# Pacing two side streams by the matrix columns of their pieces, and two small matrix products given more rows or columns of the array

## The chip, the cores and the metric

The kernel runs on one core of a Trainium2 chip. The core has five engines with a queue each, and every queue runs its instructions in order: TensorE (PE in the profile, with its weight loads as PEld), VectorE (DVE), ScalarE (ACT), GpSimd (POOL) and SyncE (SP), which here issues the DMAs. The metric is the device time of one execution in microseconds (us). Before the change it is 24933.63 us, the median of three runs (24896.19 to 24951.63).

## The reference, cut to what matters

Sixty-four images of 96 x 28 x 28 pass through four layers, all in float32 unless a layer quantises.

- Layer 0: a router mixes four expert filters for each image; a 1x1 expansion to 576 channels, a 5x5 depthwise convolution, a squeeze gate and a 1x1 projection follow, with a residual.
- Layer 1: a normalisation, an input projection, a 3x3 depthwise convolution, and then a selective scan over the 784 positions in four directions, followed by a normalisation, a gate, an output projection and an MLP.
- Layers 2 and 3: a normalisation, mixing in the frequency domain (matrix products with cosines and sines), and a feed-forward layer with quantised operands.

The scan is the heart. For each image, direction k, channel d and state n it is

```python
dt = softplus(einsum('bkrl,kdr->bkdl', dts_r, dt_projs_w) + dt_projs_b)   # dts_r has 6 rows
hst = hst * exp(dt_t * A) + dt_t * B_t * x_t        # 784 steps
y_t = sum_n(hst * C_t)
```

## The kernel before, in words

The images are taken two at a time: 32 pairs. For each pair the scan is cut into 192 units of 128 lanes by 784 positions: 12 blocks (a direction and one of three channel tiles T) of 16 units. The method `run` writes the order of all the work out by hand; there is no scheduler behind it, so an engine's queue holds its instructions as `run` and the two generators below issue them.

**A unit** (the `recur` step of unit i) is one product on DVE, `pd = pb * u` (L903), and one scan on DVE (L907 forwards, L909 backwards). Its decays `da` are made by ACT four units ahead (`decay`, L91). POOL multiplies the result with `cs` (L986). After each group of four units PE sums them over the states into `yp` (`collect`, L925).

**pb** is the input row B spread over the lanes by PE (`spread_b`, L891). It has one buffer in the accumulator memory. A new one is needed at every fourth unit, and at every second one in the four blocks with T = 2: 64 times a pair. `spread_b` for unit i+1 is issued within unit i, so PE may only run it after DVE's product of unit i, and DVE's product of unit i+1 waits for it.

**The side streams** are generators that yield pieces of work for other pairs, woven into the units of the scan: stream a (`first_half`: layer 0 and layer 1 up to the inputs of the scan) for the pair after, stream b (`second_half`: the end of layer 1 and layers 2 and 3) for the pair before. The first pair's a runs alone ahead of the scan, the last pair's b alone after it. A piece ends with `yield 0`, the last one of a **window** with `yield 1`; stream a has 135 windows and b 153. Each stream has one accumulator bank (`bank_a`, `bank_b`), so a piece's next product waits until ACT or DVE has emptied the bank. Work that a piece wants to happen later, such as a DVE operation that reads its product, is put down with `after(n, run)` and issued at the start of the n-th window after it. Such DVE operations are L383 (the Newton step of a normalisation), L787, L1081, L1093, L1291 and L662.

The pace before is by count. From unit 6 of a pair on, each stream gets at most one window a unit, and `due` allows it while its share of windows is below its share of units. In the unit two ahead of a new pb (`fresh(i + 2)`, the **quiet** unit) a window is allowed only when the stream is four windows behind:

```python
quiet = fresh(i + 2)
due = lambda v: v.window * (per - 8) < (n - 5 - QUIET * quiet) * v.windows
advance([v for v in streams if not v.over and due(v)])
```

What is left at unit 191 is run out by `finish`.

**dt's projection** is in `first_half`, `steps`: for each of four directions and three tiles, two products (L824) of 12 weight rows (partitions 96 to 107) by 128 columns, each moving 12 x 392 values: 24 a pair. ACT empties each (Exp, then Ln for both halves), one bank for all. The 12 rows are written to a row tile by ACT at partitions 96 to 107 after the product L779; partitions 0 to 63 of the same tile hold remainders of B. **The centring** in `norm` (L358) and in `feed_forward` (L1313) multiplies 96 rows by the 96 x 96 matrix `center`, 32 products a pair.

A float32 product appears as two matmul records and moves each column four times; a product with 32 output rows shares the array with three others.

Of the kernel before, what the change touches and what calls it, by code (L numbers as in the profile page):

```python
# [73 lines left out]
QUIET = 4  # L74
# [49 lines left out]
class Stream:  # L124


    def __init__(self, pieces, windows):
        self.pieces, self.windows, self.window, self.later, self.over = pieces, windows, 0, {}, False
# [4 lines left out]

    def piece(self):

        if self.over:
            return False
        more = next(self.pieces, None)
        self.over = more is None
        return more == 0  # L140

    def begin(self):
        self.window += 1
        for run in self.later.pop(self.window, []):
            run()


def advance(streams):

    for v in streams:  # L150
        v.begin()
    going = list(streams)
    while going:
        going = [v for v in going if v.piece()]


class Model:
# [3 lines left out]
    def __init__(self, ctx, tc, a, out):  # L161
        self.tc, self.nc, self.a, self.out = tc, tc.nc, a, out
        self.act = Act(tc.nc)
        self.npairs = a["x"].shape[0] // 2
# [13 lines left out]
        self.setup()  # L178

# [31 lines left out]
    def setup(self):  # L211
# [48 lines left out]
        def folded(name, bias, gain, shift, pieces, w=None):  # L260
# [4 lines left out]
            for i, (rows, lo, hi) in enumerate(pieces):  # L265
                pt = fill("ab"[i % 2])
                nc.tensor.matmul(pt[rows, :1], w[:, lo:hi], shift, start=True, stop=True)
                nc.vector.tensor_add(bias[0][rows, bias[1](i)], bias[0][rows, bias[1](i)], pt[rows, :1])
            nc.vector.tensor_scalar_mul(w, w, gain)
            pt = fill("a")  # L270
            nc.tensor.matmul(pt[:C, : 4 * C], self.center, w, start=True, stop=True)
# [41 lines left out]
        for i in (2, 3):  # L313
# [7 lines left out]
            nc.tensor.matmul(pt[:C, :DI], self.center, w1[:C], start=True, stop=True)  # L321
# [29 lines left out]
    def norm(self, bank, images, sqs, rb, scratch):  # L351
# [3 lines left out]
        for b in range(2):  # L355
            for h in range(2):
                pt = self.bank(bank)
                nc.tensor.matmul(pt[:C, :HALF], self.center, images[b][:, cols(h)], start=True, stop=True)  # L358
# [3 lines left out]
        for g in range(4):  # L362
            nc.tensor.matmul(
# [44 lines left out]
    def conv_steps(self, pt, copied, rows, steps, weights, first, last):  # L408
        nc = self.nc
        for n, (x, y) in steps:  # L410
            for q in range(4):
                nc.tensor.matmul(  # L412
# [6 lines left out]
    def first_half(self, p, st):  # L419
# [23 lines left out]
        def expand(n, h):  # L443
            i, pe = order[n], bank()
            if i == 8:
                for b in range(2):
                    nc.tensor.matmul(
# [3 lines left out]
            else:  # L451
                c = i % 4
                nc.tensor.matmul(
# [17 lines left out]
        nc.tensor.matmul(ph[:24, :2], self.r_w1, pool, start=True, stop=True)  # L471
# [11 lines left out]
        for b in range(2):  # L483
            nc.tensor.matmul(pl[:, 4 * b : 4 * b + 4], hb[:, b, :], self.r_w2, start=True, stop=True)
# [36 lines left out]
        def mix(diag, of):  # L521
            pt = bank()
            for e in range(4):
# [5 lines left out]
                nc.tensor.matmul(o, diag[:, e, :], v, start=(e == 0), stop=(e == 3))  # L529
# [94 lines left out]
        for b in range(2):  # L624
            for c in range(5):
                rhs = self.mean_s[:, b : b + 1] if c == 4 else total[:, 4 * b + c : 4 * b + c + 1]
                nc.tensor.matmul(pz[:24, b : b + 1], self.se_w1[:, c, :], rhs, start=(c == 0), stop=(c == 4))
# [7 lines left out]
        for c in range(5):  # L635
            nc.tensor.matmul(pg[:, 2 * c : 2 * c + 2], se_w2[:, c, :], z, start=True, stop=True)
# [15 lines left out]
        for b in range(2):  # L652
            for h in range(2):
                pt = bank()
                for c in range(5):
                    w = self.wp_s[:, b, :] if c == 4 else wp[:, 4 * b + c, :]
                    v = src[8] if c == 4 else src[4 * b + c]
                    nc.tensor.matmul(pt[:C, :HALF], w, v[:, cols(h)], start=(c == 0), stop=(c == 4))
# [24 lines left out]
        def in_proj(T, z, h):  # L683
            base, pt = DI if z else 0, bank()
            if T < 2:
                nc.tensor.matmul(pt[:, :HALF], self.in_w[:, base : base + 128], xs[T][:, cols(h)], start=True, stop=True)
            else:
                for b in range(2):
                    nc.tensor.matmul(
# [72 lines left out]
        w_dt = k1[96:108, 1568:1952].rearrange("p (t n) -> p t n", t=3)  # L762
# [10 lines left out]
        def project_b(k):  # L773
            low[k] = self.rows_a.tile([128, L], F32, name="o")
            t, v = parts[k], low[k]
            for h in range(2):
                pt = bank()
                for T in range(3):
                    nc.tensor.matmul(  # L779
# [6 lines left out]
                act(v[96:108, cols(h)], pt[96:108, :HALF], AF.Copy)  # L786
# [9 lines left out]
        def project_c(odd):  # L796
            for h in range(2):
                pt = bank()
                for T in range(3):
                    nc.tensor.matmul(  # L800
# [15 lines left out]
        def steps(k):  # L816
# [3 lines left out]
            for T in range(3):  # L820
                dt, x = dts[T % 2], source[T]
                for h in range(2):
                    pt = bank()
                    nc.tensor.matmul(  # L824
                        pt[:, :HALF], w_dt[:, T, :], low[k][96:108, cols(h)], start=True, stop=True
# [60 lines left out]
    def spread_b(self, u):  # L886
# [3 lines left out]
        for lo, hi in SPANS:  # L890
            nc.tensor.matmul(self.pb[:, lo:hi], self.sel[:, self.image_of(u), u["g"], :], self.bs[u["k"]][:, lo:hi], start=True, stop=True)  # L891
# [20 lines left out]
    def collect(self, us):  # L912
# [5 lines left out]
        if u["k"] == 0 and u["g"] == 2:  # L918
            for lo, hi in SPANS:
                nc.tensor.matmul(  # L920
                    self.yp[:, lo:hi], self.diag_d[:, u["T"] // 2, :], self.x[:, lo:hi], start=False, stop=False
                )
        for lo, hi in SPANS:
            for j in range(4):
                nc.tensor.matmul(  # L925
# [13 lines left out]
    def run(self):  # L939
        nc, act = self.nc, self.act  # L940
        sts = [dict(p=p) for p in range(self.npairs)]
        self.rep, self.cs, self.bs, self.done, self.stored = {}, {}, {}, None, None
# [577 lines left out]
```

## Time and profile before

The profiled execution took 24965.63 us (its span is 24963.8 us, so 1.8 us lie around it), 32 us above the median of the runs.

| | value |
|---|---|
| mean granted TensorE clock | 0.804 |
| first product of the scan, from the page's start | the stretch 0 to 528 us holds stream a of the first pair alone |
| the first pair's 192 units (only a beside them) | 528 to 1147 us: 619 us |
| a pair in the middle (a and b beside it) | 5671 to 6425 us: 754 us |
| after the last unit (b alone) | 24462 to 24964 us: 502 us |
| ACT table loads | 1116 + 937, 1283 ns each |

The page lists, for each group of instructions, the line, engine, operation and tiles (output, then inputs), partitions x elements, how many, the busy time in us, the mean of one in ns, and then how long the engine stood idle ahead of them and who ended that wait. A table by stretches lists, for each stretch of time, the busy time of each engine with its count of instructions, the granted clock of TensorE (1.00 is full speed), the share of DMA and GB/s. The list of waits says who waited for whom: us in total, times, the longest.

### The profile page before, as it was taken

The numbers are of one execution on the slowest core, as the hardware profiler recorded it, in microseconds if no ns is written. First come the engines' busy times: TensorE is split into PE (matmuls) and PEld (weight loads), VectorE is DVE, ScalarE is ACT, GpSimd is POOL, SyncE is SP. The second block draws the span as 40 slices with busy tenths as digits, with TensorE's granted clock in tenths as the row PEclk, the third lists the DMA queues.
The fourth block names the chain that finished last, engine by engine and source line by source line (L and its number), as shares of the span: only waits on it lengthen the run. The fifth ranks groups of instructions, "written<-read, shape, count | busy, mean of one in ns | idle before, by whom it ended". The sixth has DMA issues, their size and how long they took to land.

```text
span 24963.8 us, 294265 instructions
## 1 busy us (share of the span) xinstructions
PE 19171.3 (77%) x102426; PEld 7075.6 (28%) x102426; DVE 19073.0 (76%) x15930; ACT 14204.9 (57%) x19706; POOL 15593.0 (62%) x9446
## 2 busy tenths in 40 slices
PE   5677777777777787777877777877777777777866
PEld 2232222232222232222322222322222322222322
DVE  1877877877877777777778777777777778787782
ACT  2565555555565655555655555655556555556542
POOL 1666666666666666666666666666666666666662
PEclk7788878788887788877888878888787888887865
DMA  4655555555555555555555555555555555555531
GB/s 127 202 176 178 180 182 171 173 175 184 178 179 173 174 171 180 181 171 172 172 178 178 181 171 174 173 179 180 178 175 173 174 183 178 173 177 176 171 124 37
DMA packets 1733050, 4263.16 MB, mean 171 GB/s; under 512 B 203140, under 2 KB 415396, under 8 KB 1731465
## 3 DMA queue, kind: packets, MB, share of 16 engines
q1 hardware_dynamic: 1731564, 4244.33, 54.8%
q8 instruction: 812, 13.30, 0.2%
q14 instruction: 674, 5.52, 0.1%
HBM read 3206.80 MB, written 882.59 MB: 164 GB/s over the span
## 4 chain that ended last, share of the span: by engine, by line
PE 46%; DVE 24%; ACT 16%; issue 5%; DMA 4%; SPq 2%; POOL 1%; DVEq 0%; ACTq 0%; POOLq 0%
PE bank_a L412 11%; DVE pd L903 7%; DVE h L907 7%; PE yp L925 6%; ACT slot L91 5%; DVE h L909 5%; PE bank_a L824 3%; ACT da L91 3%; DMA k<-padded 2%; ACT L91 2%; PE bank_b L1268 2%; PE bank_b L1206 2%; PE pb L891 2%; PE bank_b L358 2%; PE bank_a L779 2%
## 5 line engine op out<-in xcount | busy, mean ns | idle before, releaser
L986 POOL TENSOR_TENSOR h<-h,cs 128x784 f32<-128x784 f32 x6144 | 11389.8, 1860 | 5865.7 <-DVE h L909 1840.6
L903 DVE TENSOR_TENSOR pd<-pb,u 128x784 f32<-128x784 f32 x6144 | 6013.6, 979 | 2466.6 <-PE pb L891 2235.7
L91 ACT ACTIVATE da<-dt,c_A_logs 128x784 f32<-128x784 f32 x6144 | 5602.0, 940 | 2102.8 <-DVE h L907 1252.0
L907 DVE TENSOR_TENSOR_SCAN h<-da,pd 128x784 f32<-128x784 f32 x3072 | 5488.2, 1787 | 375.6 <-DVE pd L903 14.8
L909 DVE TENSOR_TENSOR_SCAN h<-da,pd 128x784 f32<-128x784 f32 x3072 | 5487.9, 1786 | 334.5 <-DVE pd L903 4.2
L412 PE MATMUL bank_a<-k,t 128*32 128x392 f32 x36864 | 3790.1, 540 | 411.6 <-DMA k<-padded 259.7
L925 PE MATMUL yp<-h,c_gather 128*32 128x512 f32 (+1 forms) x24576 | 3326.7, 636 | 186.0 <-POOL h L986 180.6
L91 ACT ACTIVATE slot<-bank_b 99x384 f32<-99x384 f32 (+4 forms) x2624 | 1286.1, 490 | 2779.9 <-PE bank_b L358 773.9
L891 PE MATMUL pb<-bsl,c_sel 96*128 96x512 bf16 (+1 forms) x4096 | 1221.4, 386 | 1424.7 <-DVE pd L903 1393.6
L412 PEld LDWEIGHTS bank_a<-k,t 128*32 128x32 f32 x36864 | 1071.2, 114 | 2531.2 <-issue 2340.2
L925 PEld LDWEIGHTS yp<-h,c_gather 128*32 128x32 f32 x24576 | 824.6, 129 | 2841.1 <-issue 2331.1
L91 ACT ACT_TABLE_LOAD x1116 | 1431.8, 1283 | 28.9 <-PE bank_a L412 3.3
L824 PE MATMUL bank_a<-o,k 12*128 12x392 f32 x1536 | 1031.1, 763 | 383.1 <-ACT k L91 187.2
L87 ACT ACT_TABLE_LOAD x937 | 1202.2, 1283 | 17.4 <-PEq L1509 0.7
L891 PEld LDWEIGHTS <-c_sel 96*128 96x128 bf16 x4096 | 314.8, 103 | 2594.0 <-DVE pd L903 1448.3
L91 ACT ACTIVATE o<-bank_a,bn_b,bn_s 128x392 f32<-128x392 f32 x576 | 390.1, 677 | 1123.0 <-PE bank_a L412 1112.4
L1206 PE MATMUL bank_b<-c_fwd,slot 99*96 99x197 f32 (+1 forms) x4096 | 910.9, 371 | 137.7 <-DVE slot L1229 63.6
L779 PE MATMUL bank_a<-r,k 128*108 128x392 f32 x1536 | 760.1, 626 | 314.1 <-DVE o L787 308.7
L91 ACT ACTIVATE slot<-bank_b,c_l_mix 96x393 f32<-96x393 f32 x768 | 467.0, 641 | 854.6 <-PE bank_b L1206 643.5
L358 PE MATMUL bank_b<-slot,c_center 96*96 96x392 f32 x1280 | 676.7, 616 | 289.0 <-ACT slot L91 158.1
L1268 PE MATMUL bank_b<-c_inv,slot 99*96 99x394 f32 x2048 | 863.7, 571 | 13.8 <-ACT slot L91 13.8
L412 PE MATMUL bank_a<-k,cv_diag 96*32 96x392 f32 x4608 | 659.7, 710 | 253.3 <-DMA k<-padded 194.8
(232 smaller groups left out, 22964.3 us busy)
## 6 DMA issues: line engine op xcount, KB each, us to landing
cs<-crow SPq DMA_DIRECT2D x2048, 392.0 KB
dt<-dt SPq DMA_DIRECT2D x1536, 392.0 KB
u<-u SPq DMA_DIRECT2D x1536, 392.0 KB
k<-padded SPq DMA_DIRECT2D x2304, 256.0 KB
padded<-pad SPq DMA_DIRECT2D x384, 592.0 KB
u<-k SPq DMA_DIRECT2D x384, 392.0 KB
k<-padded SPq DMA_DIRECT2D x576, 224.0 KB
out<-o SPq DMA_DIRECT2D x288, 392.0 KB
```

The source lines that it names most:

```text
L91: self.nc.scalar.activation(out, in_, func, **kw)
L412: nc.tensor.matmul(pt[32 * q : 32 * q + 32, :HALF].rearrange("p (h w) -> p h w", w=HW), weights(q, n), copied[:rows, q, y : y + 14, x : x ...
L779: nc.tensor.matmul(pt[:108, :HALF], w_b[:, k, T, :], source[T][:, cols(h)], start=(T == 0), stop=(T == 2))
L824: nc.tensor.matmul(pt[:, :HALF], w_dt[:, T, :], low[k][96:108, cols(h)], start=True, stop=True)
L891: nc.tensor.matmul(self.pb[:, lo:hi], self.sel[:, self.image_of(u), u["g"], :], self.bs[u["k"]][:, lo:hi], start=True, stop=True)
L903: nc.vector.tensor_mul(pd[:, :L], self.pb[:, :L], self.rep[(u["p"], u["blk"], "u4", u["j"])])
L907: nc.vector.tensor_tensor_scan(h, da, pd[:, :L], 0.0, ALU.mult, ALU.add)
L909: nc.vector.tensor_tensor_scan(h[:, ::-1], da[:, ::-1], pd[:, L - 1 :: -1], 0.0, ALU.mult, ALU.add)
L925: nc.tensor.matmul(self.yp[32 * j : 32 * j + 32, lo:hi], self.gather, us[j]["h"][:, lo:hi], start=first, stop=last)
L986: nc.gpsimd.tensor_mul(v["h"], v["h"], self.cs[self.key(v)])
L1206: nc.tensor.matmul(pt[:C, lo:hi], folded[k][:, c, at], self.fwd[:, 2 * k + c, : hi - lo], start=(c == 0), stop=(c == 1),)
L1268: nc.tensor.matmul(pt[:C, : 2 * NF].rearrange("p (a n) -> p a n", a=2), zo[b][:, 4 * part + n, :], m, start=(n == 0), stop=(n == 3),)
```

## The change

1. **Counting.** A helper `mm` issues every matmul and adds its columns to `self.work`: four for each float32 column, one otherwise, divided by four for products of up to 32 output rows and by two up to 64.
2. **Pacing.** `debt` is a running estimate of the columns that PE has still to do: each unit adds what was issued and takes off UNIT = 6800. A stream goes on piece by piece only while the debt is below ROOM = 3600 (a quarter of it in a quiet unit), or while the stream is more than LATE = 4 windows late. A window may so be spread over several units; a stream may run up to one window early. Stream a starts at unit 0 of a pair instead of 6; b still starts at 6.
3. **dt's projection** uses 108 weight rows: `dt_w` is padded with zeros to partitions 0 to 95, and all of partitions 0 to 107 of the row tile are the moving operand. ACT's copy fills partitions 64 to 107 instead of 96 to 107.
4. **The centring** uses 128 columns: `center` is padded with 32 zero columns; what reads the bank still reads 96 rows.

The diff, cut to its core (every other hunk only puts `self.mm` for `nc.tensor.matmul`):

```diff
-QUIET = 4
+LATE, UNIT, ROOM = 4, 6800, 3600
 class Stream:
-    def begin(self):
-        self.window += 1
-        for run in self.later.pop(self.window, []):
-            run()
+    def begin(self):
+        if not self.open:
+            self.open = True
+            self.window += 1
+            for run in self.later.pop(self.window, []):
+                run()
     def piece(self):
         more = next(self.pieces, None)
         self.over = more is None
-        return more == 0
+        self.open = more == 0
+        return self.open
+    def mm(self, out, weights, moving, **kw):
+        self.nc.tensor.matmul(out, weights, moving, **kw)
+        groups = 4 if out.shape[0] <= 32 else 2 if out.shape[0] <= 64 else 1
+        self.work += int(np.prod(out.shape[1:])) * (4 if moving.dtype == F32 else 1) / groups
...
-                nc.tensor.matmul(pt[:C, :HALF], self.center, images[b][:, cols(h)], start=True, stop=True)
+                self.mm(pt[:, :HALF], self.center, images[b][:, cols(h)], start=True, stop=True)
...
-        w_dt = k1[96:108, 1568:1952].rearrange("p (t n) -> p t n", t=3)
+        w_dt = k1[:108, 1568:1952].rearrange("p (t n) -> p t n", t=3)
-                act(v[96:108, cols(h)], pt[96:108, :HALF], AF.Copy)
+                act(v[64:108, cols(h)], pt[64:108, :HALF], AF.Copy)
-                        pt[:, :HALF], w_dt[:, T, :], low[k][96:108, cols(h)], start=True, stop=True
+                        pt[:, :HALF], w_dt[:, T, :], low[k][:108, cols(h)], start=True, stop=True
...
+        def advance(streams, room):
+            for v in streams:
+                v.begin()
+            while streams:
+                going = []
+                for v in streams:
+                    if room(v):
+                        if v.piece():
+                            going.append(v)
+                        self.debt += self.work
+                        self.work = 0
+                streams = going
...
-            if u and n >= 6:
-                quiet = fresh(i + 2)
-                due = lambda v: v.window * (per - 8) < (n - 5 - QUIET * quiet) * v.windows
-                advance([v for v in streams if not v.over and due(v)])
+            self.debt = max(0, self.debt + self.work - UNIT)
+            self.work = 0
+            if u:
+                late = {v: (n + 1 - v.start) * v.windows / (per - 2 - v.start) - v.window for v in streams}
+                limit = ROOM / 4 if fresh(i + 2) else ROOM
+                due = sorted((v for v in streams if not v.over and (v.open or late[v] > -1)), key=lambda v: -late[v])
+                advance(due, lambda v: self.debt < limit or late[v] > LATE)
```

## The prediction

> **What bounds the kernel now.** I read the page first: the busy line, and the groups of the scan.
>
> ```profile
> PE 19171.3 (77%) x102426; PEld 7075.6 (28%) x102426; DVE 19073.0 (76%) x15930; ACT 14204.9 (57%) x19706; POOL 15593.0 (62%) x9446
> ...
> L903 DVE TENSOR_TENSOR pd<-pb,u 128x784 f32<-128x784 f32 x6144 | 6013.6, 979 | 2466.6 <-PE pb L891 2235.7
> ...
> L907 DVE TENSOR_TENSOR_SCAN h<-da,pd 128x784 f32<-128x784 f32 x3072 | 5488.2, 1787 | 375.6 <-DVE pd L903 14.8
> L909 DVE TENSOR_TENSOR_SCAN h<-da,pd 128x784 f32<-128x784 f32 x3072 | 5487.9, 1786 | 334.5 <-DVE pd L903 4.2
> ```
>
> No engine is full. DVE carries the chain of the scan: a unit is 0.979 + 1.787 = 2.77 us, so a pair's 192 units are 531 us of pure scan. A middle pair takes 754 us (5671 to 6425), the first pair, without stream b, 619 us. What lies between is DVE's side work and DVE's waits. Next I read the list of waits of that middle pair, DVE alone (us in total, times, longest).
>
> ```profile
> DVE pd L903 <- PE pb L891: 73.3, 27, 8.5
> DVE slot L383 <- ACT slot L91: 15.4, 5, 8.8
> DVE slot L1093 <- PE bank_b L1121: 14.4, 4, 7.3
> DVE o L787 <- ACT o L91: 9.0, 4, 3.6
> DVE slot L1291 <- PE bank_b L1268: 5.2, 2, 3.6
> DVE slot L1081 <- PE bank_b L1037: 3.7, 2, 3.4
> DVE slot L1081 <- PE bank_b L1042: 3.1, 1, 3.1
> DVE slot L1081 <- DMA k<-padded: 3.1, 1, 3.1
> DVE r L662 <- PE bank_a L658: 2.0, 2, 1.0
> ```
>
> The reader sees 73.3 us of waiting for pb and 55.9 us (the other eight lines) for side results: 129 us in all, close to the gap between the two pairs. Both kinds end on PE's queue: pb stands behind side pieces, and a piece stands behind ACT, which empties its only bank. The same list for 6370 to 6427, where stream a makes dt, has one line, pb, with 19.5 us in 5 waits. The table by stretches says why.
>
> ```profile
> 6200.00:6220.00 20.00, 14.71 (x120) 6.00 (x118) 16.81 (x13) 13.92 (x19) 13.36 (x8) 0.99 0.66 194
> 6400.00:6420.00 20.00, 15.24 (x39) 4.36 (x31) 13.13 (x11) 15.20 (x25) 10.40 (x7) 0.50 0.55 183
> ```
>
> The first number after the span is PE's busy time, the third from the end the granted clock. PE is as busy in both, yet one runs at 0.99 and the other at 0.50. In the first PE runs mostly 96-row convolution products, four side by side; in the second mostly L824, with 12 of 128 rows. From the timeline of PE, one L824 product (two records) at full and at half clock:
>
> ```profile
> 6388.39 0.92 PE L824 MATMUL bank_a<-o,k 12*128 12x392 f32 x2 [0.68 <-ACT t L91]
> 6412.08 1.67 PE L824 MATMUL bank_a<-o,k 12*128 12x392 f32 x2 [0.68 <-ACT k L91]
> ```
>
> **The change part by part**, per middle pair; stream a stands beside 31 of the 32 pairs, stream b beside 31.
>
> *dt with 108 rows.* The moving columns stay the same. At half clock a window of two products costs 2 x (1.67 + 0.68) = 4.7 us, against 2.77 us of DVE work a unit, so pb falls behind; at full clock it is 2 x (0.92 + 0.68) = 3.2 us. In the stretch 6370 to 6427 about eight of the L824 products stand at 1.67: 8 x 0.75 = 6 us; three sums L925 at 2.84 against 1.52 us elsewhere: 4 us; the small products and the three pb beside them (0.83 or 0.86 against 0.49): 3 us. That is 13 of the 19.5 us of pb waits. Ends: 19.5 us won if all go; 3 us lost if the clock stays. The latter is the weight DMA: it grows from 12 to 108 rows, nine times the bytes, and PE's 93.9 us of waits for it (2.9 a pair) could double. I take 13 won and 1 lost for the DMA. A new wait on DVE's remainder (L787, rows 0 to 63) costs nothing: it is issued four or more windows earlier.
>
> The Trainium skill, "TensorE: Matmul & The Clock Gate", Part 1 (What's actually happening), says the clock follows how busy PE was lately. Taken as busy time that speaks against this edit: PE was busy 15.24 of 20 us at 0.50, rows would not matter, and the sum would lose its 13 us. The two stretches above contradict that reading, so the measurement decides. The same page, Part 3 (What overlaps and what doesn't), has weight loads overlap running products only when their row groups differ, which 108 rows would end. L453, 96 rows by 128 columns, takes 0.93 us for its two records at full clock, beside L824's 0.92, so the sum by the row has no charge for it.
>
> *The centring with 128 columns.* 32 products a pair, the same moving columns; L358's loads take 180 ns with 96 columns and L453's 198 with 128, so 64 x 18 ns = 1.2 us of loads, mostly ahead of their products. What it wins is bounded by L358's records at half clock (about 0.9 against 0.54 us for one, some 28% of them): 32 x 0.28 x 0.7 = 6 us of PE, off DVE's path. I take 0.
>
> *Pacing and DVE's side waits.* I counted float32 columns in the order in which the program issues them, side pieces alone, in a middle pair. Both kernels issue 754,836. Before, 27 of the 192 units get more than 9,300 (four us at full clock by the row: 3,136 columns of L412 take 1.53 us), after it 12. The longest single lump falls from 14,720 to 12,576, and the first 24 units get 59,234 instead of 46,690, since stream a starts six units earlier. A DVE operation put down with `after(1)` comes one unit, some 2.9 us, after its product; behind 9,300 columns it must wait. In the trace two thirds of the side waits (38 us) start within two units of such lumps. If they shrink with the lumps, 38 x 15/27 = 21 us go; I take 18. Ends: 55.9 won, 11 lost. The loss is ACT table loads: the program has 2331 instead of 2053, 8.7 more a pair at 1.283 us, and they stand in ACT's queue ahead of what L383 and L787 wait for. ACT is busy 446 of 754 us, so I charge a quarter in the sum, 3 us.
>
> *Pacing and pb.* Outside the dt stretch pb costs 73.3 - 19.5 = 54 us. Before, 42 of 64 quiet units issue no side work, after it 15; their mean rises from 1,372 to 3,013 columns, 0.80 us more at full clock, 1.49 at half (2.84 us for the same 3,136). The cover: PE itself waits 1393.6 us for DVE ahead of L891, 0.68 us for each of 2048. Ends: 54 won, 51 lost (64 x 0.80). The two nearly cancel; smoother units and a later pile-up ahead of pb leave, I judge, 4 us won, nearest to no change. Behind a late pb stand DVE's next unit, POOL's L986 and the sum L925.
>
> *Rest.* `finish` at unit 191 has two windows left of each stream instead of one: one unit of chained work, 3 us lost. The side streams' DMAs on SP keep their order and number. In the head, 24 L824 products, some half at half clock, lie on the path: 12 x 0.75 = 9 us won. The tail (clock 0.54, one chain with no scan beside it) stays.
>
> Sum: -13 + 1 - 18 + 3 - 4 + 3 = -28 us a pair, x 31 = -868, with the head -877. The profiled execution took 24965.6 us, so 24,089; it lies 32 us above the median, so I predict **24,057 us**.
>
> **The rivals.**
>
> - *Pacing only renames the count.* By the program's own counters, in 70% of units at least one stream is over four windows late and so ignores the debt. For it: both streams trail their share by nearly four windows most of the pair. Against: the lumps do get fewer. Then only dt pays: -13 + 1 + 3 + 3 = -6 a pair, -195 with the head: 24,740.
> - *The clock doesn't follow the rows.* For it: L779, with 128 rows, also has many slow records (mean 626 ns). Then -18 + 3 - 4 + 3 + 1 = -15 a pair: 24,470.
> - *An even load holds the clock everywhere.* The mean clock is 0.804, and a PE that no longer idles for several units may keep it. Then half of the 54 us of pb goes too, -27 instead of -4: -51 a pair: 23,340.
> - *The quiet units are missed* (the other side). Extra columns ahead of pb delay it at two thirds of the 64 spreads by 0.80 us: +34 a pair, with -13 + 1 - 18 + 3 + 3 = -24 from the rest: +10, 25,235. It decides from +0.38 us a spread (24/64). For it: the cover of 0.68 us is a mean, and 554 waits hold all of it.
>
> **How the numbers follow.** Forecast 0.38; count renamed 0.20; clock unmoved 0.10; even load 0.14; quiet missed 0.13; nothing to be seen 0.05. About 0.2% (50 us) is what a measurement of this kernel can tell from no change. Faster: 0.38 + 0.20 + 0.10 + 0.14 = 0.82, less 0.02 for the weak end of the renamed count: 0.80; same 0.05 + 0.02 = 0.07; slower 0.13. The range, 23,300 to 25,000 us, takes in all but the slower case and the far ends.
>
> **What would show it.** dt: L824 near 560 ns a record, clock near 1.0 where it stands, pb waits there under 7 us. Pacing: L383, L1081 and L1093 waits down by a third or more. Quiet units: L903's wait for pb, 2235.7 us now, would rise outside dt if the rival holds. The mean clock should rise above 0.804 to some 0.84. The prediction is wrong if pb's total doesn't fall below 1,900 us, or if the side waits stay.

## The result, and the profile after

The changed kernel takes **25175.65 us** (median of 4 runs, 25157.35 to 25190.23) against 24942.63 us for the kernel before beside it: ratio 1.0095, 95% interval 1.0078 to 1.0113. It is slower by 233 us where 877 us less were forecast. The profiled execution took 25163.06 us, its span is 25161.1 us, the mean granted clock 0.809 (0.804 before). Where single executions of a kernel took far longer than the rest (two in experiment e4, one in e7), the time given is the median of the others.

The page after, its busy line and the group of the scan's first product. The line numbers move by 1 to 21; all matmuls now come from the helper, L179.

```profile
PE 18834.0 (75%) x102426; PEld 7334.8 (29%) x102426; DVE 18859.4 (75%) x15930; ACT 14564.5 (58%) x19984; POOL 15587.3 (62%) x9446
...
L906 DVE TENSOR_TENSOR pd<-pb,u 128x784 f32<-128x784 f32 x6144 | 6013.8, 979 | 2799.9 <-PE pb L179 2501.1
```

First, the waiting of DVE for pb rose from 2235.7 to 2501.1 us. Second, DVE's busy time *fell*, from 19073.0 to 18859.4 us, with the same 15930 instructions. So DVE stood idle for 25161.1 - 18859.4 = 6302 us against 5891 before: the change cost 411 us of waiting, and 214 us of shorter DVE instructions hid half of it. The forecast had nothing of the second.

The list of waits of the same middle pair as before, now 5718 to 6483 us (765 us, before 754), DVE alone:

```profile
DVE pd L906 <- PE pb L179: 81.2, 30, 7.2
DVE slot L1114 <- PE bank_b L179: 17.7, 4, 5.5
DVE o L790 <- ACT o L92: 10.9, 5, 4.1
DVE slot L1258 <- ACT slot L92: 6.6, 3, 3.4
DVE slot L386 <- ACT slot L92: 5.8, 5, 2.2
DVE k L386 <- ACT k L92: 4.4, 1, 4.4
DVE slot L1102 <- PE bank_b L179: 4.1, 3, 1.8
...
DVE rw L491 <- PE bank_a L179: 3.2, 1, 3.2
DVE gate L641 <- PE bank_a L179: 2.9, 1, 2.9
DVE gate L646 <- ACT gate L92: 2.8, 1, 2.8
...
DVE slot L1249 <- ACT slot L92: 2.3, 3, 1.2
```

Of the three that the forecast named, L386 (L383 before) fell from 15.4 to 5.8 us and L1102 (L1081) from 9.9 to 4.1, and L1114 (L1093) rose from 14.9 to 17.7. L1258, L386 on k, L491, L641, L646 and L1249, which together waited for about 1 us before, now wait for 22 us. The side waits moved to other steps.

The table by stretches, in the part where stream a makes dt (before 0.59 and 0.50 in the third number from the end):

```profile
6440.00:6460.00 20.00, 12.55 (x29) 4.50 (x33) 15.01 (x11) 16.02 (x27) 10.95 (x6) 0.68 0.56 188
6460.00:6480.00 20.00, 11.71 (x39) 3.89 (x35) 10.01 (x8) 13.95 (x23) 12.64 (x8) 0.59 0.67 212
```

The clock is a little higher there, far from the forecast, near 1.0. The groups by form name dt's products after the change, 742 ns a record against 763 before, and their waits for the weight DMA, 168.9 us against 93.9:

```profile
L179 PE MATMUL bank_a<-o,k 108*128 108x392 f32 x1536 | 996.6, 742 | 484.1 <-ACT t L92 171.9 <-DMA k<-in_dt_w 168.9 <-ACT k L92 136.0
```

### The profile page after: what moved, and what is told of

Its sections match the earlier page's. It is cut to its first block, busy times and chain, and to the rows that moved or that the text cites. A ratio compares the mean times of both kernels' runs of the same rounds, so it can differ in the third digit from the quotient of the medians.

```text
span 25161.1 us, 294525 instructions
## 1 busy us (share of the span) xinstructions
PE 18834.0 (75%) x102426; PEld 7334.8 (29%) x102426; DVE 18859.4 (75%) x15930; ACT 14564.5 (58%) x19984; POOL 15587.3 (62%) x9446
## 4 chain that ended last, share of the span: by engine, by line
PE 40%; DVE 20%; ACT 20%; issue 6%; DMA 5%; POOL 2%; SPq 1%; DVEq 0%; ACTq 0%; POOLq 0%
PE bank_a L179 18%; PE bank_b L179 16%; ACT slot L92 6%; DVE pd L906 6%; DVE h L910 6%; PE yp L179 5%; ACT da L92 5%; DVE h L912 4%; ACT L92 2%; ACT L88 2%; PE pb L179 1%; POOL h L1004 1%; ACT k L92 1%; ACT o L92 1%; ACT pad L92 1%
## 5 line engine op out<-in xcount | busy, mean ns | idle before, releaser
L906 DVE TENSOR_TENSOR pd<-pb,u 128x784 f32<-128x784 f32 x6144 | 6013.8, 979 | 2799.9 <-PE pb L179 2501.1
L179 PE MATMUL bank_a<-k,t 128*32 128x392 f32 (+3 forms) x38144 | 4215.1, 547 | 310.6 <-ACT pad L92 227.8
L179 PE MATMUL yp<-h,c_gather 128*32 128x512 f32 (+1 forms) x24576 | 3019.4, 606 | 163.9 <-POOL h L1004 163.7
L179 PEld LDWEIGHTS bank_a<-k,t 128*32 128x32 f32 (+1 forms) x38144 | 1391.2, 121 | 2719.8 <-issue 2224.4
L179 PE MATMUL pb<-bsl,c_sel 96*128 96x512 bf16 (+1 forms) x4096 | 1207.8, 382 | 1169.5 <-DVE pd L906 1019.0
L179 PE MATMUL bank_b<-slot,c_center 96*128 96x392 f32 x1792 | 1044.9, 672 | 691.3 <-DVE slot L1336 372.7
L179 PEld LDWEIGHTS yp<-h,c_gather 128*32 128x32 f32 x24576 | 781.7, 125 | 2510.5 <-issue 2078.3
L179 PE MATMUL bank_b<-c_fwd,slot 99*96 99x197 f32 (+1 forms) x4096 | 1041.5, 410 | 526.0 <-DVE slot L1250 444.8
L179 PE MATMUL bank_a<-o,k 108*128 108x392 f32 x1536 | 996.6, 742 | 484.1 <-ACT t L92 171.9
L179 PE MATMUL bank_a<-r,k 128*108 128x392 f32 (+1 forms) x2304 | 1073.2, 595 | 374.2 <-DVE o L790 253.6
L179 PE MATMUL bank_b<-slot,slot 96*128 96x392 f32 (+1 forms) x1536 | 806.6, 629 | 407.9 <-ACT slot L92 374.3
L179 PEld LDWEIGHTS bank_b<-c_fwd,slot 99*96 99x96 f32 x4096 | 787.1, 202 | 856.1 <-issue 615.2
L179 PEld LDWEIGHTS <-c_sel 96*128 96x128 bf16 x4096 | 356.1, 105 | 2254.5 <-issue 1279.9
```

Source lines behind the costliest of these rows:

```text
L179: self.nc.tensor.matmul(out, weights, moving, **kw)
L906: nc.vector.tensor_mul(pd[:, :L], self.pb[:, :L], self.rep[(u["p"], u["blk"], "u4", u["j"])])
```

## The experiments

All ratios are to the kernel before on the same chip, whose medians lie between 24936 and 24943 us. "Idle" is DVE's: span less busy time of the profiled execution. The edits are cut to the lines that tell; "..." stands for what belongs to them (e1: the other two places of dt's rows and the padded weights; e2: the second product and the padded matrix).

### One part alone

Three theories. P: the pacing costs and the matrices give nothing. R: the matrices win what was forecast, the pacing costs more. C: the matrices themselves cost.

```diff
@@ e1: the kernel before, with @@
-        w_dt = k1[96:108, 1568:1952].rearrange("p (t n) -> p t n", t=3)
+        w_dt = k1[:108, 1568:1952].rearrange("p (t n) -> p t n", t=3)
...
@@ e2: the kernel before, with @@
-                nc.tensor.matmul(pt[:C, :HALF], self.center, images[b][:, cols(h)], start=True, stop=True)
+                nc.tensor.matmul(pt[:, :HALF], self.center, images[b][:, cols(h)], start=True, stop=True)
...
@@ e3: the changed kernel, with both matrices as before @@
-        w_dt = k1[:108, 1568:1952].rearrange("p (t n) -> p t n", t=3)
+        w_dt = k1[96:108, 1568:1952].rearrange("p (t n) -> p t n", t=3)
-                self.mm(pt[:, :HALF], self.center, images[b][:, cols(h)], start=True, stop=True)
+                self.mm(pt[:C, :HALF], self.center, images[b][:, cols(h)], start=True, stop=True)
...
```

> The kernel before with dt's 108 weight rows alone; order and pacing are those of before. Theory P (the pacing costs time, the rows and columns do next to nothing): 24,900 to 24,980 us, no measurable change, and about half of the L824 records still at half clock. Theory R (the rows raise the clock as the prediction said, and the pacing costs more than was seen): 24,940 - 400 = 24,540 us, with the L824 records near 560 ns and the pb waits of the dt stretch falling from about 19 us to under 7 us a pair. Theory C (the added rows cost time, by the larger weight load and its DMA): 25,050 us or more.

Measured: 24851.02 us, 0.9965 (0.9952 to 0.9979): 90 us won.

> The kernel before with the centring's 128 columns alone. Theory P: 24,900 to 24,980 us, no measurable change. Theory R: up to 100 us faster, by a higher clock around the normalisations. Theory C: slower by some 50 to 150 us, because each of the 2048 weight loads is longer and the product waits for it.

Measured: 24982.19 us, 1.0013 (1.0005 to 1.0022): 42 us lost.

> The changed kernel with dt's 12 rows and the centring's 96 columns put back: the pacing alone. Theory P: 25,130 to 25,220 us, all of the loss, with waits for pb near 2,500 us. Theory R: 25,550 us, the pacing's loss without the gain of the rows. Theory C: at or below the kernel before, 24,900 us.

Measured: 25340.84 us, 1.0161 (1.0148 to 1.0174): 400 us lost. DVE idles for 6448 us, 557 more than before.

The pacing costs. dt's rows win 90 us, about a quarter of the 381 that were forecast for them (31 x 12, and 9 in the head), and the centring loses a little. With the pacing the two matrices together win 165 us (25,341 to 25,176), without it 36 (e10 below). None of the three theories is right as it stood; P is nearest. e1 is the fastest kernel of this study, faster than the kernel before and than the changed one.

### Inside the pacing

Theories: S, stream a's start at unit 0; L, the 278 more table loads; D, the holding back by the debt, with the missed quiet units.

```diff
@@ e4: the changed kernel, with the quiet unit kept @@
-                advance(due, lambda v: self.debt < limit or late[v] > LATE)
+                advance(due, lambda v: late[v] > 2 * LATE if quiet else self.debt < ROOM or late[v] > LATE)
@@ e5: the changed kernel, with stream a's start (b still starts at 6) @@
-            if u and n == 0:
+            if u and n == 6:
...
@@ e6: the changed kernel, with @@
-LATE, UNIT, ROOM = 4, 6800, 3600
+LATE, UNIT, ROOM = 12, 6800, 3600
@@ e7: the kernel before, with 278 table loads more, of the table that is there already @@
...
+                nc.scalar.preload_act_table_set(EXP_LN)
@@ e8: the changed kernel, with the debt ignored @@
-                advance(due, lambda v: self.debt < limit or late[v] > LATE)
+                advance(due, lambda v: True)
```

> The changed kernel with the quiet unit kept: in the unit two ahead of a new pb a stream goes on only when it is over eight windows late, whatever the debt. If the pacing loses because side pieces are issued right ahead of pb, pb's waits fall from 2,501 to 2,000 us or less and the time to 24,900 us or less. If the pacing loses elsewhere (other alignments of the streams, ACT's table loads), the time stays within 60 us of 25,170 us, or rises because more windows are pressed into the other units.

Measured: 25328.72 us, 1.0157 (1.0144 to 1.017), 153 us more than the changed kernel. Its idle time did fall, to 6191 us, but its DVE instructions took 276 us longer. By the trace, the wait for pb fell from unit 8 of a pair on, from 77.8 to 56.3 us a pair, and rose in the first eight units from 3.5 to 26.0. So the missed quiet units do cost waiting for pb, but keeping them in this way wins no time.

> The changed kernel with stream a starting at unit 6 of a pair, as before the change, instead of 0. The program then has 2085 ACT table loads instead of 2331 (before: 2053). Theory S (the early start sets stream a against other stages of stream b, and the first eight units, 8.5 us slower a pair, are dear): 24,900 to 25,000 us. Theory L (the table loads carry the loss): also near 24,950 us, since the loads are nearly gone. Theory D (holding pieces back by the debt, and the missed pb, carry the loss): 25,100 to 25,250 us, as after.

Measured: 24969.86 us, 1.0014 (1.0006 to 1.0023): 206 of the 233 us are gone.

> The changed kernel with LATE = 12 instead of 4: a stream obeys the debt until it is twelve windows late. 2529 table loads. Theory D: the debt has more say, so more of the same loss, 25,300 us or more. If instead the override by lateness is what spoils the pacing, the waits for pb fall below 2,236 us and the time to 24,900 us or less. Theory L: 198 loads more than after, 25,300 to 25,450 us.

Measured: 25526.9 us, 1.0234 (1.0221 to 1.0247). A debt that is obeyed more is dearer: what was held back comes out at the pair's end, ahead of the next pair's first new pb, at unit 4. DVE's wait for pb is 2922.1 us; in the first eight units of a pair it is 42.8 us, against 3.5 in the changed kernel.

> The kernel before with 278 more ACT table loads, as many as the change adds: one is issued about every 22 units, where the table is already the one for Exp, so nothing else changes. It adds 278 x 1.283 = 357 us of ACT. Theory L: 25,150 to 25,300 us, most of the pacing's 400 us. Theories S and D: under 100 us slower, 24,940 to 25,040 us, since ACT is busy for 57% only.

Measured: 25071.04 us, 1.0052 (1.0039 to 1.0065): 130 us for 278 loads, 0.47 us each (0.35 to 0.58 by the interval), of the 1.283 us that one takes on ACT. That is more than S and D allowed and less than L. The expectations that follow take 0.56 us, from 25096.75 us, the median of all six; with 0.47 theory L's lower ends lie lower still.

> The changed kernel with the debt left out of the decision: a stream gets its next window each unit as soon as it is less than one window early, with no quiet unit and no window split. Rows, columns and the start of a at unit 0 stay. 2425 table loads. Theory D: the loss goes, 24,850 to 24,950 us. Theory S: 25,100 to 25,250 us, no better than after. Theory L: 94 loads more than after, 25,250 us or more.

Measured: 25506.17 us, 1.0226 (1.0212 to 1.0239). The wait for pb is 3354.7 us, so the debt did take 854 us of it away, in a kernel that starts stream a at unit 0 and has no quiet units.

### The start, under both paces

The kernel before with both new matrices is the missing corner of a table: old pace or debt, stream a from unit 6 or from unit 0. In e9 the line shown is that of stream a; b still starts at 6.

```diff
@@ e10: the kernel before, with both matrices as in e1 and e2 @@
@@ e9: e10, with @@
-            if u and n == 6:
+            if u and n == 0:
...
-                due = lambda v: v.window * (per - 8) < (n - 5 - QUIET * quiet) * v.windows
+                due = lambda v: v.window * (per - 2 - v.start) < (n + 1 - v.start - QUIET * quiet) * v.windows
```

> The kernel before with both the 108 weight rows and the 128 centring columns, and the old count pace untouched: the corner (old pace, stream a from unit 6) of a table of four, whose other corners are e5 (pace by debt, a from unit 6: +29 us against before), the changed kernel (pace by debt, a from unit 0: +233) and e9 below (old pace, a from unit 0). Its table loads are the 2053 of before. The parts alone gave -90 (rows) and +42 us (columns). If they add, 24,893 us, ratio 0.998. If the columns cost only where the rows are missing, 24,850, ratio 0.9965. The theory that the debt itself is worth something with a from unit 6 (it cuts the waits beside pb from 80 to 73 us in a pair) needs this corner to be slower than e5, 24,970 or more; the theory that the debt costs by itself needs it at 24,900 or less, with e5 then 70 us or more above it.

Measured: 24901.08 us, 0.9986 (0.9977 to 0.9995).

> As e10, but stream a starts at unit 0 of its pair, as in the changed kernel, under the old count pace with its quiet units (stream b still from unit 6). The program has 2549 table loads, 496 more than e10 and 218 more than the changed kernel. Theory S with L (the early start costs under any pace, by the table loads that it adds, at the 0.56 us each that e7 showed): e10 + 280, near 25,170 us, ratio near 1.009. Theory D (the start costs only under the debt's pace, which holds streams back): e10 +- 30, near 24,890, ratio 0.998. A middle value would split the 205 us of the start between the two.

Measured: 25321.56 us, 1.0161 (1.0147 to 1.0175).

| | a from unit 6 | a from unit 0 |
|---|---|---|
| by count, quiet units | 24,901 (e10) | 25,322 (e9) |
| by debt | 24,970 (e5) | 25,176 (the change) |

The start costs 420 us under the old pace and 206 under the debt. With the old start the debt costs 69 us, with the new one it wins 146. So the start is what made the changed kernel slower than before, and the debt is worth nothing by itself: the matrices (-36), the debt with the old start (+69) and the start (+206) add up to 239 of the measured 233. The trace of e5 beside that of e10 shows why the debt wins nothing. DVE's side waits fall from 57.7 to 51.7 us a pair, as they were meant to, and its wait for pb rises from 70.2 to 77.9. In the changed kernel both are dearer than in e5, 61.5 and 81.3. It looked as if the table loads might carry the start (2549 in e9 against 2053). Two starts were chosen to break that: the loads don't grow with an earlier start.

```diff
@@ e13: e9, with @@
-            if u and n == 0:
+            if u and n == 2:
@@ e14: e9, with @@
-            if u and n == 0:
+            if u and n == 9:
```

> As e9 (both rows and columns, the old count pace), but stream a starts at unit 2 of its pair: 2205 table loads in the program, 152 more than e10 (2053) and 344 fewer than e9 (2549, 25,322 us). Theory L (the loads that the shifted windows add): 152 loads at between 0.56 us (e7's price) and 0.85 us (e9 less e10, 420 us over 496 loads) give e10's 24,901 + 85 to 129, so 24,985 to 25,030 us, ratio 1.002 to 1.004. Theory S (an early start costs by the units by which it is early, 420 us for six): four units early, 24,901 + 280, near 25,180 us, ratio 1.010.

Measured: 25453.71 us, 1.0207 (1.0193 to 1.0221).

> As e10, but stream a starts at unit 9, three units later than in the kernel before: 2583 table loads, 530 more than e10 and the most of any start from 0 to 9 but one. Theory L: 24,901 + 530 x 0.56 to 0.85, so 25,200 to 25,350 us, ratio 1.010 to 1.016. Theory S (only an early start costs): no dearer than e10, 24,850 to 24,930 us, ratio 0.997 to 1.000, but for the little that three fewer units make stream a denser (135 windows in 181 units and not 184).

Measured: 25413.45 us, 1.0191 (1.0177 to 1.0205).

Both theories fall. e13 has few loads and is the dearer one; e14 starts later than before and is as dear. The next question was what a start shifts: the streams against each other (theory M), or against the scan (theory G).

```diff
@@ e15: e10, with both streams from unit 8 @@
-            if u and n == 6:
+            if u and n == 8:
@@ e16: e10, with stream a from unit 6, and stream b @@
-            if u and n == 6:
+            if u and n == 8:
```

> As e10 (both rows and columns, the old count pace), with both streams from unit 8 instead of 6: their windows keep their places beside each other (both go through the same fraction of their windows at every unit) and move against the scan's units. 2237 table loads, 184 more than e10. Theory M (what meets what in the two streams sets the time): e10's 24,901 + at most 184 x 0.56 = 103, so 24,900 to 25,010 us. Theory G (the place of the windows against the scan's own steps sets it, and a start at 6 is a good place): 24,901 + 400 to 550, as e9, e13 and e14, so 25,300 to 25,450 us.

Measured: 24891.51 us, 0.9981 (0.9972 to 0.999).

> As e10, with stream a from unit 6 and stream b from unit 8, two units later: stream a keeps its place against the scan, stream b moves against both. The loads are e10's 2053. Theory M: the two streams meet otherwise, 24,901 + 300 to 550, so 25,200 to 25,450 us. A theory that only stream a's place counts (against the scan, or its tables): 24,880 to 24,950 us. Theory G allows either for b, since b's own place against the scan moves too.

Measured: 25426.65 us, 1.0197 (1.0183 to 1.0211), with exactly e10's 2053 table loads.

Under the old pace M holds for the one shift tried: both moved alike by two units costs nothing, b alone moved by two costs 526 us. Two runs asked whether that carries over to the changed kernel's pace.

```diff
@@ e17: the changed kernel, with @@
-            if u and n == 0:
+            if u and n == 6:
-            elif u and n == 6 and i // per > 0:
+            if u and n == 12 and i // per > 0:
@@ e18: the changed kernel, with @@
-            if u and n == 0:
+            if u and n == 8:
-            elif u and n == 6 and i // per > 0:
+            if u and n == 8 and i // per > 0:
```

> The changed kernel with stream a from unit 6 and stream b from unit 12: a's lead of six units over b is kept, but a starts where it did before. 2145 table loads. Theory M (the lead sets which steps of the two streams meet, and so the time): as the changed kernel, 25,176 us +- 100. Theory S (what cost 206 us was a's early start): as e5, 24,970 +- 50. Theory L (table loads): e5 + 60 loads x 0.56 to 0.85 = 25,000 to 25,020.

Measured: 25715.84 us, 1.0312 (1.0297 to 1.0326).

> The changed kernel with both streams from unit 8: no lead, as in e5, but two units later. 2331 table loads, exactly the changed kernel's number. Theory M: as e5, 24,970 us +- 60. Theory L: as the changed kernel, 25,176, or e5 + 246 x 0.56 = 25,108 at the least. Theory G (the places against the scan): anything up to 25,400.

Measured: 25707.01 us, 1.0312 (1.0298 to 1.0326).

It doesn't carry over. e18 differs from e5 only by two units for both streams and costs 737 us more; e17 is as dear. Under the debt the windows are also cut and delayed by what the scan itself issues, so a shift of both changes which pieces meet as well; that this is the reason was argued, not shown. What is shown: with the same instructions, but for some table loads, the place at which the two streams' pieces stand, by start and pace, moves the time between 24,892 and 25,716 us.

### Where the place of a step shows: DVE's instructions themselves

The same groups of DVE in e10, in e16 and after the change: first a step with both inputs in SBUF, the core's working memory, then a step that reads the accumulator (bank_b), then a sum of nine columns, again with both inputs in SBUF. The columns after the bar are busy us and the mean ns of one.

e10:

```profile
L1237 DVE SCALAR_TENSOR_TENSOR slot<-slot,slot 96x393 f32<-96x393 f32 x256 | 191.4, 748 | 32.5 <-ACT slot L91 32.1
L1229 DVE SCALAR_TENSOR_TENSOR slot<-bank_b,l_neg,slot 96x393 f32<-96x393 f32 x256 | 159.6, 623 | 24.0 <-DVE slot L1228 1.4
...
L607 DVE TENSOR_TENSOR total<-sums 128x9 f32<-128x9 f32 x32 | 34.8, 1087 | 175.6 <-ACT o L91 175.6
```

e16:

```profile
L1243 DVE SCALAR_TENSOR_TENSOR slot<-slot,slot 96x393 f32<-96x393 f32 x256 | 426.0, 1664 | 87.5 <-ACT slot L91 84.9
...
L1235 DVE SCALAR_TENSOR_TENSOR slot<-bank_b,l_neg,slot 96x393 f32<-96x393 f32 x256 | 159.6, 623 | 23.7 <-DVE slot L1234 0.9
...
L607 DVE TENSOR_TENSOR total<-sums 128x9 f32<-128x9 f32 x32 | 102.0, 3186 | 211.7 <-ACT o L91 211.7
```

The changed kernel:

```profile
L1258 DVE SCALAR_TENSOR_TENSOR slot<-slot,slot 96x393 f32<-96x393 f32 x256 | 215.9, 843 | 203.0 <-ACT slot L92 202.6
...
L1250 DVE SCALAR_TENSOR_TENSOR slot<-bank_b,l_neg,slot 96x393 f32<-96x393 f32 x256 | 159.6, 623 | 23.3 <-DVE slot L1249 0.5
...
L610 DVE TENSOR_TENSOR total<-sums 128x9 f32<-128x9 f32 x32 | 5.6, 174 | 178.6 <-ACT o L92 178.6
```

Nine columns take 174, 1087 or 3186 ns; the step that reads the accumulator takes 623 ns in all three. The timelines show what stands beside such a sum, first in e16, then in the changed kernel (start, duration, engine):

```profile
6153.37 3.65 POOL L992 TENSOR_TENSOR h<-h,cs 128x784 f32<-128x784 f32 x2
6153.67 3.38 DVE L607 TENSOR_TENSOR total<-sums 128x9 f32<-128x9 f32 x1 [1.20 <-ACT o L91]
```

```profile
6118.75 3.78 POOL L1004 TENSOR_TENSOR h<-h,cs 128x784 f32<-128x784 f32 x2
6120.44 0.18 DVE L610 TENSOR_TENSOR total<-sums 128x9 f32<-128x9 f32 x1
```

In e16 DVE's sum ends with POOL's second multiplication, in the changed kernel it came 0.16 us before POOL's first ended. In e10, 125 of the 224 runs of L384 begin while POOL works; there one takes the rest of POOL's instruction plus 0.42 us (1485 ns left, 1906 ns; 584 ns left, 1007 ns), the others 567 ns.

Not every step on SBUF alone waits. In e16 those with two inputs do, and a copy with one (L499: 1.73 us on average where it begins beside POOL, 0.17 elsewhere), while reciprocals (L496) and reductions (L491) that begin beside POOL take their usual 166 and 161 ns.

The Trainium skill, "SBUF — State Buffer", section "SBUF: two separate sides", says that a DVE instruction with two SBUF inputs and a GpSimd instruction that reads SBUF exclude each other for a whole instruction. The rows agree; that the waiting one may have to let a second GpSimd instruction pass (3.38 us), they add.

I summed, over DVE's side steps that touch only SBUF, what each took above the 5th percentile of its line: 453 us before, 225 after the change, 483 in e10, 675 in e16, 216 in e18; 95% or more of it in steps that began while POOL was at work. For the steps that read the accumulator the sum is 20 to 30 us in all of them. Where nearly all runs of a line wait, the 5th percentile is itself a wait. Above the fastest run of each group the sums are 495, 272, 526, 789 and 258 us, and 564 in e5, and their differences are nearly those of DVE's busy time: -223 against -214 from before to after, +262 against +258 from e10 to e16, -306 against -287 from e5 to e18. So the longer DVE instructions are these waits.

The busy lines of e10 and e16, and those of e5 and e18, then split the prices of e16 and e18.

```profile
PE 18824.0 (76%) x102426; PEld 7110.1 (29%) x102426; DVE 19107.3 (77%) x15930; ACT 14216.0 (57%) x19706; POOL 15608.1 (63%) x9446
PE 19086.5 (75%) x102426; PEld 7267.8 (29%) x102426; DVE 19365.4 (76%) x15930; ACT 14213.6 (56%) x19706; POOL 15583.6 (61%) x9446
```

```profile
PE 18724.9 (75%) x102426; PEld 7167.3 (29%) x102426; DVE 19131.0 (77%) x15930; ACT 14234.9 (57%) x19738; POOL 15579.9 (62%) x9446
PE 19024.0 (74%) x102426; PEld 7374.9 (29%) x102426; DVE 18844.4 (73%) x15930; ACT 14573.3 (57%) x19984; POOL 15593.4 (61%) x9446
```

e16 over e10: span 25411.5 against 24875.8, of which 258 us are longer DVE instructions (19365.4 against 19107.3) and 278 us idle time. e18 over e5: 696 us of span, made of 982 us more idle time and 287 us less in the instructions. The change over e10: 533 us more idle, 248 us less busy. The two parts go their own ways; neither alone ranks the kernels.

Where e18's idle time stands, the lists of waits say, e5 first:

```profile
DVE slot L386 <- ACT slot L92: 238.5, 69, 49.9
DVE slot L1114 <- PE bank_b L179: 265.7, 119, 22.3
```

```profile
DVE slot L386 <- ACT slot L92: 669.8, 158, 49.9
DVE slot L1114 <- PE bank_b L179: 521.4, 121, 22.4
```

These two and L790 (293.1 to 431.7 us) and L1312 (282.4 to 389.3) make up 932 of the 982 us; the wait for pb hardly moves (2407.7 and 2427.3). So in e18 it is side steps that come to wait for their inputs, and not pb.

### dt's clock

Does the granted clock follow how long the array is busy, or how much of it is at work? Both runs issue each of dt's products twice, into the same bank with the same values; only the rows differ.

```diff
@@ e11: e1, and e12: the kernel before, each with @@
-                    nc.tensor.matmul(
+                    for _ in range(2): nc.tensor.matmul(
...
```

> The kernel before with the 108 weight rows alone, and each of dt's products issued twice in a row into the same bank (the second writes the same values again), so that the array is at work for longer in each turn of the chain product, exponential, product. Two theories of what the granted clock follows. By occupancy (weight rows x columns x moving columns over time): one product in the chain at half clock is some 23% of the array's capacity, two are some 32% at half clock and 51% at full clock, so the records of dt's product at half clock should fall from 0.51 of all (108 rows once) to 0.35 or less. By busy time alone: the same fall, and the same in e12. The time: 48 more products in a pair at 0.56 us each at full clock are 27 us if all lie on the path, 0 if all are hidden by the decay steps; less 48 x 0.16 x 0.37 = 3 us that the clock gives back. So from 24,750 to 25,600 us; near 25,000 if a fifth of them is on the path.

Measured: 25237.38 us, 1.013 (1.0114 to 1.0145).

> The kernel before with its 12 weight rows, each of dt's products issued twice in a row into the same bank. Theory occupancy: two 12-row products are under 6% of the array's capacity even at full clock, so the share of dt's records at half clock stays at 0.56 or above (0.563 once, before). Theory busy time (the clock follows how long the array is busy, whatever its rows): the share falls as in e11, to 0.35 or less. The time: 48 more products in a pair at 0.76 to 0.92 us each, up to 44 us if all are on the path: from 24,940 to 26,300 us; by occupancy slower than e11 by at least 100 us, by busy time as e11.

Measured: 25748.19 us, 1.033 (1.0316 to 1.0344).

The groups by form of PE: e1, e11, e12, and the kernel before.

```profile
L824 PE MATMUL bank_a<-o,k 108*128 108x392 f32 x1536 | 979.3, 730 | 460.7 <-ACT k L91 188.3 <-DMA k<-in_dt_w 162.2 <-ACT t L91 108.0
```

```profile
L825 PE MATMUL bank_a<-o,k 108*128 108x392 f32 x3072 | 1546.5, 637 | 475.8 <-DMA k<-in_dt_w 229.6 <-ACT k L91 152.7 <-ACT t L91 91.9
```

```profile
L825 PE MATMUL bank_a<-o,k 12*128 12x392 f32 x3072 | 2003.9, 795 | 278.7 <-ACT k L91 93.1 <-ACT t L91 90.9 <-DMA k<-in_dt_w 83.7
```

```profile
L824 PE MATMUL bank_a<-o,k 12*128 12x392 f32 x1536 | 1031.1, 763 | 383.1 <-ACT k L91 187.2 <-DMA k<-in_dt_w 93.9 <-ACT t L91 91.5
```

The share of these records that start at half clock: 0.563 before, 0.513 with 108 rows, 0.339 with 108 rows twice, 0.725 with 12 rows twice, and 0.541 in the changed kernel. Twice the work of 12 rows makes the clock worse, twice that of 108 rows makes it better: in these runs the clock follows how much of the array is at work, and one 108-row product in a turn that waits for ACT is too little to lift it much.

## Why the prediction was wrong, point by point

- **The step that failed** is "Pacing and DVE's side waits": that 27 lumps cut to 12 take 18 us of side waits with them. Over the 29 middle pairs, from the trace, DVE's idle time elsewhere than ahead of pb's product, short gaps included, went from 80.1 to 82.7 us a pair (+2.6). The waits behind lumps did go, and by the amount forecast: by the same count of columns, side waits in the two units after a unit of more than 9,300 columns fell from 38.1 to 19.5 us a pair. But those behind units with less rose from 20.0 to 41.5, for which the sum had no term: other steps came to stand badly. With stream a at unit 6 (e5) the idle time fell to 73.1, which is 7.0 won, still not 18. (9,300 columns are 4.5 us by the prediction's own row, 9,300 / 3,136 x 1.53, not four.)
- **Stream a's start at unit 0** had no price in the sum; it stood there only as columns moved to the first 24 units. e5 and e9 price it at 206 and 420 us. It is no price of an early start, nor of its table loads, as e13 and e14 show: under the old pace it is the new place of the two streams against each other (e15, e16), and nothing in the profile of before tells its price.
- **pb outside dt**, -4 us with bounds of -54 and +51: in the units ahead of the last 15, DVE's idle time ahead of pb's product rose from 60.5 to 73.0 us a pair, +12.5, inside the bounds (2.4 of it are waits for other inputs). "Smoother units" was a wrong ground for the sign. My own count of columns hardly tells a wait: unit by unit its correlation with the following pb wait is 0.10 before and 0.14 after.
- **dt with 108 rows**, -13 + 1: e1 won 90 us, 2.9 a pair. In the last 15 units, where dt stands, DVE's idle time ahead of pb's product stayed (17.6 us a pair before, 17.3 in e1, 16.0 after the change), as the clock hardly rose. The two stretches, convolution at 0.99 and dt at 0.50, showed rightly that rows count, but not from what share on. For the weight DMA, at 1, PE's waits rose by (162.2 - 93.9) / 31 = 2.2. The 9 us in the head can't be told: it took 527.8 us before, 525.2 after the change and 518.3 in e1, but 516.0 in e3, which has the old rows.
- **The centring**, 0: 42 us lost by itself (1.4 a pair), 50 beside the rows (e10 less e1). Why is open.
- **Table loads**, +3: 8.7 x 0.47 = 4.1 by e7's price.
- **finish**, +3: the last eight units took 37.3 us a pair against 38.5, so nothing.
- **DVE's busy time** was taken as fixed, and fell by 214 us, 6.9 a pair. With it the sum closes: idle ahead of pb's product +10.9, other idle +2.6, busy -6.9 make +6.6, and a pair went from 755.4 to 762.1 us.

Of the rivals, "the quiet units are missed" gave 25,235, near the time, but that is luck: pb's part rose by a third of its 34 us, its sum still had the 18 us of side waits won, and with the quiet units kept (e4) the time grew. "Pacing only renames the count" was right that the debt wins nothing, and wrong that it then costs nothing (69 us with the old start); obeying it more (e6) was worse. "An even load holds the clock everywhere" fails at the mean clock, 0.809. "The clock doesn't follow the rows" is refuted by e11 and e12, although in this edit it hardly moved. The test named in the prediction, pb's total under 1,900 us, failed at 2501.

Open is why both streams from unit 6 is a good place under both paces, and which pieces meet where the side steps come to wait. Every fast kernel here has both streams started together, but e18 shows that this isn't enough.

## What to carry to other kernels

Where hand-woven streams share in-order queues, the start of a stream is part of the tuning: moving one by two units of 192 cost 2% with the same instructions, so try each scheduling change with the old starts first, and several starts. Price a smoother load by the waits that it creates at other steps, not only by those that it removes; and split a difference into the bounding engine's idle time and its busy time before explaining either, since here they went opposite ways. A zero-padded matrix product lifted the clock here clearly only where the array then also worked more of the time (108 rows twice, and hardly once).

## What the runs showed of the hardware that was not expected

- A DVE step with two inputs in SBUF, or a copy like L499, waits for the GpSimd instruction that is running, 0.15 us of work taking up to 3.40, and the profile books that as DVE's busy time; reciprocals and reductions (166 and 161 ns beside GpSimd) and steps that read the accumulator (623 ns everywhere) are untouched.
- The clock granted to TensorE fell when it was kept busy with few rows: 0.725 of dt's records at half clock with 12 rows twice, 0.563 with 12 rows once. The Trainium skill, "TensorE: Matmul & The Clock Gate", Part 1 (What's actually happening), puts the clock down to how busy TensorE was; here the rows decide it.
- A table load that changes nothing but ACT's time cost 0.47 us of this kernel's time, under half of its 1.283 us.
